# Two reorderings in a four-layer kernel: the ternary linear's third block, and the first gate and up products of a SwiGLU

## The chip, the cores and the metric

The kernel runs on one core of a Trainium2 chip. The metric is the device time of one execution in microseconds (us). The time of a kernel is the median of its runs. One execution was taken by the hardware profiler, and all rows that are shown come from it.

## The reference

The input is 2 x 1024 tokens of 512 channels, in float32. Four layers follow one another, each as `x = layernorm(x + layer(x))`:

1. a state-space layer (input projection, short causal convolution, scan, gated output projection),
2. a ternary linear layer: `out = (x @ W) * scale`, with W of -1, 0 and 1, then each row scaled by tanh of its norm and clipped to norm 0.99,
3. a recurrence layer:
   `y = gelu(x @ w_y + b_y)`, `c = causal_conv(x @ w_x + b_x)`, `i = sigmoid(c @ w_ig + b_ig)`, `a = exp(-8 * sigmoid(c @ w_ag + b_ag) * softplus(a_param))`, `h[t] = a[t] * h[t-1] + sqrt(1 - a[t]^2) * i[t] * c[t]`, `out = (h * y) @ w_out + b_out`,
4. a SwiGLU layer with integer weights (less 128, scaled per output channel): `out = (silu(x @ Wg) * (x @ Wu)) @ Wd`, hidden size 2048.

The change touches the border between layers 2 and 3, and the one between layers 3 and 4.

## The kernel before, in words

**Blocks.** The 2048 tokens are four blocks of 512 (`NBLK` = 4, two per sequence). `X[b]` holds block b in SBUF, 128 tokens x 4 groups `j` x 512 channels. The 512 channels are four chunks `k` of 128. A product needs the block with channels on the partitions, so each block is first transposed by TensorE: 16 transposes of 128 x 128 into four PSUM tiles `pt`, each copied to SBUF by ScalarE. A product against float32 data is a matmul that appears as two instructions in the profile. Layers 2 and 4 use a cheaper form (`exact`): the activations are split into a rounded high part (a cast on ScalarE) and the low rest (a subtraction on VectorE), and each k takes one matmul of each part.

**PSUM.** All PSUM tiles come from one pool of eight banks, `ps.tile([P, 512], F32, tag="mm")`. Every product, every transposed chunk and every accumulating output takes one bank until its last reader is done.

**Order.** Python traces the program, and the framework's scheduler then fixes one order per engine. In a model of the run, each engine takes, of the instructions that are ready and can get their buffer, the one that was traced first. An instruction traced earlier thus has a higher rank, but a later one that is ready goes ahead of it when it isn't. On the chip each engine keeps the order that was fixed and waits on semaphores. Generators with `yield` and the helper `weave(main, fill, plan)` set the order of tracing: after each step of `main`, as many steps of `fill` as `plan` says.

**Border of layers 2 and 3.** `linear(b)` is the ternary layer of block b. Its four steps are: transposes (L219), high cast `wu` (L223) and low part `wd` (L224); two of the four token groups, each eight matmuls (L896), a scaling on VectorE (L900) and a square with row sum on ScalarE (L902); the other two groups; and norm, tanh (L910) and the update of `X[b]` (L906 to L920) with a layernorm on GpSimd (L244). The pieces `wu` and `wd` have one buffer, so a block's casts wait until the block before has been multiplied. `linear(0)` and `linear(1)` are woven into the end of layer 1, whose last block is stored to DRAM (L735) and read back (L935). `branches(b)` begins layer 3 for block b: transposes (L219) with copies by ScalarE (L228), then four products with `w_x` (L947) each followed by bias, convolution and carry, then four with `w_y` and a gelu. Its transposed block lies in memory that layer 1 held. Here `branches(0)` is the `main` of a `weave` and `linear(2)`, `linear(3)` the `fill`, one step of fill after each of the first eight steps.

**Border of layers 3 and 4.** For each block, `recurrence(b)` does the two gate products, the activations and the scan; `project_back(b)` multiplies the result by `w_out` (32 matmul instructions, L1024, into four banks `po`), adds the bias (`r`, L1029, VectorE) and adds it to `X[b]` (L1030, GpSimd), with a layernorm for all but the last block. In the loop `project_back(b - 1)` stands behind `recurrence(b)`. Behind the loop stand `by_channel(0, X, pieces)`, the transposes (L877), high casts (L880) and low parts `lo` (L882) of block 0 for the SwiGLU, and `project_back(3)`. Then the pool of layer 4 is opened, and `hidden(0)` multiplies block 0 by the first 128 columns of gate and up (16 matmuls, L1098, into two banks `pgu`), with silu (L1105), product (L1107) and its split for the down-projection (L1121).

All of this is traced twice, `later_layers(True)` and, behind a test of the weights, `later_layers(False)`; with these inputs the second is jumped over.

Of the kernel before, what the change touches and what calls it, by code (L numbers as in the profile page):

```python
# [16 lines left out]
P = 128  # L17
# [3 lines left out]
NK = D // P  # L21
# [16 lines left out]
def model_kernel(ctx: ExitStack, tc: tile.TileContext, t: dict, out: bass.AP):  # L38
    nc = tc.nc
# [15 lines left out]
    def bank(name):  # L55
        return ps.tile([P, 512], F32, tag="mm", name=name)
# [198 lines left out]
    def weave(main, fill, plan, rest=True):  # L255

        for i, _ in enumerate(main):
            for _ in range(plan[i] if i < len(plan) else 0):
                next(fill, None)
        for _ in fill if rest else ():  # L260
            pass
# [475 lines left out]
    H, before, st = None, None, {}  # L737
    own, coming = head(0, st), {}
    g, ahead = gates(0, st), head(1, coming)
# [8 lines left out]
    for b in range(NBLK):  # L748
        if b:
            g, coming = gates(b, st), {}  # L750
# [54 lines left out]
    GK = GW // P  # L805
# [3 lines left out]
    def later_layers(exact, last=None):  # L809
# [62 lines left out]
        def by_channel(b, X, pieces):  # L872

            for k in range(NK):
                pt = bank("pt")
                for j in range(NJ):
                    nc.tensor.transpose(  # L877
                        pt[:, j * P : (j + 1) * P], X[b][:, j, k * P : (k + 1) * P], ident
                    )
                nc.scalar.copy(pieces[0][:, k, :], pt)  # L880
                if exact:
                    nc.vector.tensor_tensor(  # L882
                        pieces[1][:, k, :], pt, pieces[0][:, k, :].bitcast(F32), ALU.subtract
                    )

        def linear(b):

            xT = transposed(ep, b, X, tags=("wu0", "wd0") if exact else ("wu0",), split=exact)
            yield
            o = ep.tile([P, NJ, D], F32, tag="wF", name="o" + suffix)  # L890
            ssq = sp.tile([P, NJ], F32, tag="ssq", name="ssq")
            for j in range(NJ):
                po = bank("po")
                for k in range(NK):
                    for x in xT:
                        nc.tensor.matmul(  # L896
                            po, x[:, k, j * P : (j + 1) * P], wf[:, k, :],
                            start=(k == 0 and x is xT[0]), stop=(k == NK - 1 and x is xT[-1]),
                        )
                nc.vector.tensor_tensor(o[:, j, :], po, f0s, ALU.mult)  # L900
                junk = ep.tile([P, GW], mybir.dt.bfloat16, tag="junk", name="junk2")
                nc.scalar.activation(junk, o[:, j, :], AF.Square, accum_out=ssq[:, j : j + 1])  # L902
                if j % 2:
                    yield
            norm = sp.tile([P, NJ], F32, tag="norm", name="norm")
            nc.scalar.activation(norm, ssq, AF.Sqrt)  # L906
            v = sp.tile([P, NJ], F32, tag="v", name="v")
            nc.vector.tensor_scalar(v, norm, 1e-7, None, ALU.max)
            f = sp.tile([P, NJ], F32, tag="f", name="f")
            nc.scalar.activation(f, v, AF.Tanh)  # L910
            nc.vector.tensor_scalar(v, v, 1e-7, None, ALU.add)
            nc.vector.reciprocal(v, v)
            nc.vector.tensor_tensor(f, f, v, ALU.mult)
            nc.vector.tensor_tensor(norm, norm, f, ALU.mult)
            nc.vector.tensor_scalar(norm, norm, 1e-7, None, ALU.max)
            nc.vector.reciprocal(norm, norm)
            nc.vector.tensor_scalar(norm, norm, 0.99, 1.0, ALU.mult, ALU.min)
            nc.vector.tensor_tensor(f, f, norm, ALU.mult)
            for j in range(NJ):
                nc.vector.scalar_tensor_tensor(  # L920
                    X[b][:, j, :], o[:, j, :], f[:, j : j + 1], X[b][:, j, :],
                    ALU.mult, ALU.add,
                )
            layernorm(X[b], engine=nc.gpsimd)
            yield
# [10 lines left out]
        for i, name in ((2, "w_ig"), (3, "w_ag"), (4, "w_out")):  # L936
            nc.sync.dma_start(w1[:, i], w_sources[name])


        with tc.tile_pool(name="rec" + suffix, bufs=1, side="right", reuse_waits="tile") as rp:  # L940
            carry = rp.tile([P, NK, 3], F32, tag="carry", name="carry1")
# [11 lines left out]
            def branches(b, st):  # L953

                xT = transposed(rp, b, X, by_act=True)[0]
                yield
                cv = st["cv"] = rp.tile([P, NK, TB], F32, tag="cv", name="cv", bufs=2)
                y = st["y"] = rp.tile([P, NK, TB], F32, tag="y", name="y", bufs=2)
                for m in range(NK):
                    pm = product(0, m, xT)  # L960
                    xpad = rp.tile([P, 3 + TB], F32, tag="xpad", name="xpad1", bufs=2)
                    if b % BPS == 0:
                        nc.gpsimd.memset(xpad[:, 0:3], 0.0)
                    else:
                        nc.gpsimd.tensor_copy(xpad[:, 0:3], carry[:, m, :])
                    nc.scalar.activation(xpad[:, 3:], pm, AF.Identity, bias=bx[:, m : m + 1])
                    if b % BPS < BPS - 1:
                        nc.gpsimd.tensor_copy(carry[:, m, :], xpad[:, TB : TB + 3])
                    nc.vector.tensor_scalar(
                        cv[:, m, :], xpad[:, 3:], cw1[:, m, 3:4], cb1[:, m : m + 1],  # L970
                        ALU.mult, ALU.add,
                    )
                    causal_conv(cv[:, m, :], xpad, cw1[:, m, :])
                    yield
                for m in range(NK):
                    pm = product(1, m, xT)
                    nc.scalar.activation(y[:, m, :], pm, AF.Gelu, bias=by[:, m : m + 1])
                    yield
# [41 lines left out]
            def project_back(b, y):  # L1020
                for j in range(NJ):
                    po = bank("po")
                    for k in range(NK):
                        nc.tensor.matmul(  # L1024
                            po, y[:, k, j * P : (j + 1) * P], w1[:, 4, k, :],
                            start=(k == 0), stop=(k == NK - 1),
                        )
                    r = rp.tile([P, D], F32, tag="t2", name="r1", bufs=4)
                    nc.vector.tensor_tensor(r, po, bout, ALU.add)  # L1029
                    nc.gpsimd.tensor_tensor(X[b][:, j, :], X[b][:, j, :], r, ALU.add)  # L1030

                if b + 1 < NBLK:
                    layernorm(X[b])

            st = {}
            weave(branches(0, st), itertools.chain(linear(2), linear(3)), (1,) * 8)
            bout = row("L1_attn_b_out", D, c1, nc.sync, "scale")
            wg, wu, wd = ([weights(ep, which, 0)] for which in ("wg", "wu", "wd"))
            ys = []
# [11 lines left out]
                for tag in (("wF", "lo") if exact else ("wF",))  # L1051
            ]
            by_channel(0, X, pieces)
            project_back(NBLK - 1, ys[-1])
            dsc = row("L1_ffn_down_scale", D, c1, nc.sync, "scale")

# [3 lines left out]
        with tc.tile_pool(name="ffn" + suffix, bufs=1, side="right", reuse_waits="tile") as fp:  # L1060
# [26 lines left out]
                            i += 1  # L1087
                        yield

            def hidden(m):  # L1090

                g, cols = m // GK, slice(m % GK * P, m % GK * P + P)
                pgu = []
                for w in (wg, wu):
                    pm = bank("pgu")
                    for k in range(NK):
                        for x in pieces:
                            nc.tensor.matmul(  # L1098
                                pm, w[g][:, k, cols], x[:, k, :],
                                start=(k == 0 and x is pieces[0]),  # L1100
                                stop=(k == NK - 1 and x is pieces[-1]),
                            )
                    pgu.append(pm)
                sg = fp.tile([P, TB], F32, tag="sg", name="sg", bufs=2)
                nc.scalar.activation(sg, pgu[0], AF.Silu, scale=gs[:, m : m + 1])  # L1105
                h = fp.tile([P, TB], F32, tag="h", name="h", bufs=2 if exact else 3)
                nc.vector.scalar_tensor_tensor(  # L1107
                    h, pgu[1], us[:, m : m + 1], sg, ALU.mult, ALU.mult
                )
                if not exact:  # L1110
                    return [h]
                hh = fp.tile([P, TB], F32R, tag="hh", name="hh", bufs=4)
                nc.scalar.copy(hh, h)  # L1113
                hl = fp.tile([P, TB], F32R, tag="hl", name="hl", bufs=4)
                nc.vector.tensor_tensor(hl, h, hh.bitcast(F32), ALU.subtract)
                return [hh, hl]
# [6 lines left out]
                            start=(m == 0 and x is h[0]), stop=(m == NF - 1 and x is h[-1]),  # L1123
                        )

            ready, check = [hidden(0)], squares()
            loads = itertools.chain(*(group(g) for g in range(1, NG)))
            for b in range(NBLK):
                final = b + 1 == NBLK
# [124 lines left out]
```

## Time and profile before

| what | us |
|---|---|
| median of 3 runs | 1148.89 |
| lowest and highest run | 1146.79, 1148.90 |
| the profiled execution | 1149.05 |
| its span, first to last instruction | 1147.2 |
| TensorE busy in the span | 1118.7 (98%) |
| VectorE busy | 678.9 (59%) |
| ScalarE busy | 459.0 (40%) |
| GpSimd busy | 361.9 (32%) |

The profiled execution's time is 1.85 us over its span. In the rows, PE is TensorE's matmuls, PEld its weight loads, DVE VectorE, ACT ScalarE, POOL GpSimd and SP the engine that issues most DMAs; `L947` is line 947 of the kernel. A timeline row has the start in us from the begin of the span, the time in us, engine, line, operation, output and inputs, shapes and count; in brackets stands the idle time of the engine ahead of it and what ended that. Neighbouring instructions of one kind are merged into one row. The end of a matmul is modelled, so that rows on PE overlap a little; the step from start to start is the price of one.

### The profile page before, as it was taken

How to read it: one execution, taken by the hardware profiler on the slowest of the kernel's cores; microseconds unless marked ns; L12 is line 12 of the kernel's file. 1: busy time of each engine (PE TensorE's matmuls, PEld its weight loads, DVE VectorE, ACT ScalarE, POOL GpSimd, SP SyncE). 2: the span in 40 equal slices, each digit the busy share in tenths (PEclk: the TensorE clock that was granted, in tenths of full speed). 3: DMA queues.
4: the chain of work that ended last, by engine and by line, in shares of the span. 5: the costliest groups of instructions: out<-in, count | busy, mean ns of one | idle time of the engine just before them, and what ended most of it. 6: DMA issues, size and time to landing. Idle time of an engine off the chain costs nothing.

```text
span 1147.2 us, 12259 instructions
## 1 busy us (share of the span) xinstructions
PE 1118.7 (98%) x4614; PEld 684.2 (60%) x4614; DVE 678.9 (59%) x1228; ACT 459.0 (40%) x700; POOL 361.9 (32%) x347
## 2 busy tenths in 40 slices
PE   8989999999999999999999999999999999999995
PEld 5455445445544555654444444448888888888884
DVE  4887896696769676863717237083328765225224
ACT  3343544463454233566654372533223223223222
POOL 1446472555248240556123212237401001001002
PEclk9999999999999999999999999999999999999998
DMA  8004002400220038112000000004501001001001
GB/s 316 20 14 167 2 1 89 166 0 37 69 113 0 38 144 234 74 31 89 1 1 0 1 0 1 0 1 128 175 1 38 1 1 37 1 1 37 1 1 40
DMA packets 32699, 59.22 MB, mean 52 GB/s; under 512 B 11808, under 2 KB 12608, under 8 KB 30072
## 3 DMA queue, kind: packets, MB, share of 16 engines
q1 hardware_dynamic: 31608, 58.21, 14.5%
q8 instruction: 38, 0.62, 0.2%
q14 instruction: 29, 0.24, 0.1%
q10 hardware_dynamic: 864, 0.14, 0.1%
q0 software_dynamic: 160, 0.01, 0.0%
HBM read 49.47 MB, written 8.68 MB: 51 GB/s over the span
## 4 chain that ended last, share of the span: by engine, by line
PE 84%; DVE 10%; ACT 4%; issue 1%; POOL 0%; DVEq 0%; ACTq 0%; POOLq 0%
PE pgu L1098 21%; PE p L947 17%; PE po L1121 10%; PE pg L323 9%; PE px L323 7%; PE po L715 6%; PE po L1024 4%; PE py L650 3%; DVE acc L251 2%; PE po L896 2%; DVE L L522 2%; PE pxt L619 1%; PE pt L219 1%; DVE xc L700 1%; PE py L642 1%
## 5 line engine op out<-in xcount | busy, mean ns | idle before, releaser
L1107 DVE SCALAR_TENSOR_TENSOR h<-pgu,L_ffn_up_scale,sg 128x512 f32<-128x512 f32 x64 | 47.9, 749 | 147.7 <-PE pgu L1098 143.7
L323 PE MATMUL px<-xT,w_in 128*128 128x512 f32 x256 | 114.6, 597 | 0.2 <-DVE over L509 0.2
L537 POOL TENSOR_TENSOR L<-L,gm 128x512 f32<-128x512 f32 x64 | 93.5, 1490 | 67.0 <-DVE bdec L532 29.4
L715 PE MATMUL po<-w_out,xc 128*128 128x512 f32 x256 | 112.5, 593 | 2.1 <-DVE L L522 2.1
L947 PE MATMUL p<-xT,w 128*128 128x512 f32 x256 | 112.1, 592 | 1.4 <-ACT xT L228 1.4
L323 PE MATMUL pg<-xT,w_in 128*128 128x512 f32 x256 | 113.4, 594 | 0.0
L947 PE MATMUL p<-cv,w 128*128 128x512 f32 x256 | 111.0, 592 | 0.0
L1121 PE MATMUL po<-wd,hh 128*128 128x512 f32 x256 | 101.3, 396 | 0.0
L1098 PE MATMUL pgu<-wF__4424,wg 128*128 128x512 f32 x256 | 101.2, 396 | 0.0
L1121 PE MATMUL po<-wd,hl 128*128 128x512 f32 x256 | 101.0, 394 | 0.0
L1098 PE MATMUL pgu<-lo__4425,wg 128*128 128x512 f32 x256 | 100.7, 393 | 0.0
L1098 PE MATMUL pgu<-lo__4425,wu 128*128 128x512 f32 x256 | 100.7, 393 | 0.0
L1098 PE MATMUL pgu<-wF__4424,wu 128*128 128x512 f32 x256 | 100.7, 393 | 0.0
L1105 ACT ACTIVATE sg<-pgu,L_ffn_gate_scale 128x512 f32<-128x512 f32 x64 | 44.0, 688 | 133.1 <-PE pgu L1098 133.0
L1113 ACT CAST hh<-h 128x512 fp32r<-128x512 f32 x64 | 39.7, 621 | 117.5 <-DVE h L1107 117.3
L715 PEld LDWEIGHTS po<-w_out,xc 128*128 128x128 f32 x256 | 48.4, 190 | 63.1 <-issue 55.7
L947 PEld LDWEIGHTS p<-cv,w 128*128 128x128 f32 x256 | 48.4, 190 | 59.8 <-issue 58.6
L947 PEld LDWEIGHTS p<-xT,w 128*128 128x128 f32 x256 | 48.4, 190 | 58.8 <-issue 55.3
L323 PEld LDWEIGHTS px<-xT,w_in 128*128 128x128 f32 x256 | 47.6, 190 | 57.8 <-issue 56.3
L1195 POOL TENSOR_TENSOR x<-x,r 128x512 f32<-128x512 f32 x12 | 15.2, 1294 | 205.9 <-DVE r L1194 205.9
L323 PEld LDWEIGHTS pg<-xT,w_in 128*128 128x128 f32 x256 | 47.4, 190 | 54.3 <-issue 53.7
L251 DVE SCALAR_TENSOR_TENSOR acc<-xpad,cols,acc 128x512 f32<-128x512 f32 x72 | 67.4, 939 | 18.5 <-ACT acc L293 14.8
(268 smaller groups left out, 1937.2 us busy)
## 6 DMA issues: line engine op xcount, KB each, us to landing
L<-decays SPq DMA_DIRECT2D x12, 1024.0 KB, 9.1
x_mid<-x SPq DMA_DIRECT2D x4, 1024.0 KB, 3.8
x<-x_mid SPq DMA_DIRECT2D x4, 1024.0 KB, 6.8
st<-in_L_ffn_gate_w_dram SPq DMA_DIRECT2D x8, 512.0 KB, 4.5
st<-in_L_ffn_up_w_dram SPq DMA_DIRECT2D x8, 512.0 KB, 4.1
st<-in_L_ffn_down_w_dram SPq DMA_DIRECT2D x8, 512.0 KB, 3.6
x<-_attn_hidden_states_dram SPq DMA_DIRECT2D x3, 1024.0 KB, 9.9
out_dram<-x SPq DMA_DIRECT2D x3, 1024.0 KB, 4.4
```

The costliest lines, as they stand in the source:

```text
L251: nc.vector.scalar_tensor_tensor(acc, xpad[:, k : k + TB], w[:, k : k + 1], acc, ALU.mult, ALU.add)
L323: nc.tensor.matmul(pm[:n, :], w_in[:, k, lo : lo + n], xT[:, k, :], start=(k == 0), stop=(k == NK - 1),)
L537: nc.gpsimd.tensor_tensor(L[:, h, :], L[:, h, :], st["gm"], ALU.mult)
L650: nc.tensor.matmul(pys[i][hh * HD : (hh + 1) * HD, q, :], dtx[q][:, 2 * i + hh, :], L[:, h, s], start=(first and q == 0), stop=(q == 1), s ...
L715: nc.tensor.matmul(po, xc[:, m, j * P : (j + 1) * P], w_out[:, m, :], start=(m == 0), stop=(m == NX - 1),)
L947: nc.tensor.matmul(pm, w1[:, i, k, m * P : (m + 1) * P], rhs[:, k, :], start=(k == 0), stop=(k == NK - 1),)
L1024: nc.tensor.matmul(po, y[:, k, j * P : (j + 1) * P], w1[:, 4, k, :], start=(k == 0), stop=(k == NK - 1),)
L1098: nc.tensor.matmul(pm, w[g][:, k, cols], x[:, k, :], start=(k == 0 and x is pieces[0]), stop=(k == NK - 1 and x is pieces[-1]),)
L1105: nc.scalar.activation(sg, pgu[0], AF.Silu, scale=gs[:, m : m + 1])
L1107: nc.vector.scalar_tensor_tensor(h, pgu[1], us[:, m : m + 1], sg, ALU.mult, ALU.mult)
L1113: nc.scalar.copy(hh, h)
L1121: nc.tensor.matmul(po[j], x[:, j * P : (j + 1) * P], wd[m // GK][:, m % GK, :], start=(m == 0 and x is h[0]), stop=(m == NF - 1 and x is h ...
```

## The change

It does two things to the order of tracing. In front of the weave of `branches(0)`, one step is taken from the fill, so that the first step of `linear(2)` is traced ahead of the first step of `branches(0)`, and every later step of the two `linear` blocks comes one step of `branches(0)` earlier. And the matmuls of gate and up are taken out of `hidden` into a function `gate_up`, which is called for m = 0 between `by_channel(0)` and `project_back(3)`; `hidden(0)` then gets the two banks handed over. No operation is added or removed.

```diff
+        def gate_up(m):
+            g, cols = m // GK, slice(m % GK * P, m % GK * P + P)
+            pgu = []
+            for w in (wg, wu):
+                pm = bank("pgu")
+                for k in range(NK):
+                    for x in pieces:
+                        nc.tensor.matmul(
+                            pm, w[g][:, k, cols], x[:, k, :],
+                            start=(k == 0 and x is pieces[0]),
+                            stop=(k == NK - 1 and x is pieces[-1]),
+                        )
+                pgu.append(pm)
+            return pgu
...
             st = {}
-            weave(branches(0, st), itertools.chain(linear(2), linear(3)), (1,) * 8)
+            rest = itertools.chain(linear(2), linear(3))
+            next(rest)
+            weave(branches(0, st), rest, (1,) * 8)
...
             by_channel(0, X, pieces)
+
+            first_hidden = gate_up(0)
             project_back(NBLK - 1, ys[-1])
...
-            def hidden(m):
+            def hidden(m, pgu=None):
+
+                pgu = pgu or gate_up(m)
...
-            ready, check = [hidden(0)], squares()
+            ready, check = [hidden(0, first_hidden)], squares()
```

More of the change, by code (lines that the diff above doesn't have):

```diff
@@ L1088, in squares @@
                         yield
-            def hidden(m):
[L1092 to L1103, printed above, removed]
+            def hidden(m, pgu=None):
+                pgu = pgu or gate_up(m)
                 sg = fp.tile([P, TB], F32, tag="sg", name="sg", bufs=2)
```

## The prediction

> **What bounds the kernel now.** The page first: TensorE is busy for 98% of the span, no other engine for over 60% (PEld overlaps PE).
>
> ```profile
> PE 1118.7 (98%) x4614; PEld 684.2 (60%) x4614; DVE 678.9 (59%) x1228; ACT 459.0 (40%) x700; POOL 361.9 (32%) x347
> ```
>
> So an edit that only moves work can gain no more than TensorE's waits. Next, the waits of TensorE: place, what it waited for, us in total, times, longest. In the two stages touched there are these:
>
> ```profile
> PE po L1024 <- DVE r L1029: 1.7, 1, 1.7
> PE p L947 <- ACT xT L228: 1.4, 1, 1.4
> PE po L896 <- DVE wd L224: 0.9, 2, 0.8
> PE pt L219 <- POOL xpad L963: 0.4, 1, 0.4
> ```
>
> That is 4.4 us, 0.38% of the time: the ceiling. What comes later has no slack to swallow a delay: in the table by stage the SwiGLU reads (length, then busy us of PE, PEld, DVE, ACT, POOL; then the granted clock)
>
> ```profile
> 800.00:900.00 100.00, 100.00 (x441) 81.56 (x441) 49.33 (x96) 27.77 (x42) 20.98 (x28) 1.00 0.19 65
> ```
>
> 100.00 of 100.00, so a microsecond lost or won on TensorE ahead of it reaches the end in full.
>
> The timeline by engine around the first stage, TensorE's rows, then ScalarE's (start, length, line; in brackets the idle time before):
>
> ```profile
> 458.90 1.17 PE L896 MATMUL po<-wfr,wu 128*128 128x512 f32 x4
> 460.22 0.50 PE L896 MATMUL po<-wfr,wd 128*128 128x512 f32 x1 [0.15 <-DVE wd L224]
> ...
> 466.73 0.49 PE L219 MATMUL pt<-ident,x 128*128 128x128 f32 x3
> 467.63 3.38 PE L219 MATMUL pt<-ident,x 128*128 128x128 f32 x29 [0.41 <-POOL xpad L963]
> 472.43 3.70 PE L947 MATMUL p<-xT,w 128*128 128x512 f32 x8 [1.41 <-ACT xT L228]
> ```
>
> ```profile
> 469.43 1.28 ACT L910 ACT_TABLE_LOAD   x1
> 470.72 0.20 ACT L910 ACTIVATE f<-v 128x4 f32<-128x4 f32 x1
> 470.83 1.05 ACT L223 CAST wu<-pt 128x512 fp32r<-128x512 f32 x2
> 471.78 2.06 ACT L228 COPY xT<-pt 128x512 f32<-128x512 f32 x4
> ```
>
> Two things are to be seen. The four `wu` matmuls at 458.90 run in a row although each group alternates `wu` and `wd`: the order on TensorE is built by readiness, a group is opened with its high part and then waits for its low part. And the 32 transposes (16 of `branches(0)`, 16 of `linear(2)`) end near 471.0, after which TensorE has nothing until the copy of `xT`. That copy starts at 471.78 because its memory held a token block: SyncE issued the store of the last block (L735) at 467.03, and only at 471.57 the load behind it (L935), which must wait for that store.
>
> The timeline of all engines around the second stage:
>
> ```profile
> 756.25 1.91 PE L877 MATMUL pt<-ident,x 128*128 128x128 f32 x16
> ...
> 759.10 0.67 DVE L1029 TENSOR_TENSOR r<-po,L_attn_b_out 128x512 f32<-128x512 f32 x1
> 759.82 14.00 PE L1024 MATMUL po<-w,y 128*128 128x512 f32 x32 [1.66 <-DVE r L1029]
> ...
> 760.27 1.94 DVE L1029 TENSOR_TENSOR r<-po,L_attn_b_out 128x512 f32<-128x512 f32 x3
> ...
> 765.90 0.66 DVE L882 TENSOR_TENSOR lo__4425<-pt,wF__4424 128x512 fp32r<-128x512 f32 x1
> ...
> 769.62 0.68 DVE L882 TENSOR_TENSOR lo__4425<-pt,wF__4424 128x512 fp32r<-128x512 f32 x1
> ...
> 773.25 0.80 PE L1098 MATMUL pgu<-wF__4424,wg 128*128 128x512 f32 x1
> ```
>
> The 1.66 us are a wait for a PSUM bank. All eight are taken: four `po` of block 2, which VectorE reads only from 759.10, and four `pt` of `by_channel`, which the subtraction L882 frees from 766.56. The first reader ends at 759.77 and the out-projection of block 3 starts at 759.82.
>
> **The change, part by part.** No instruction is added or removed and no DMA is moved; nothing passes anything on SP's or POOL's queue. The sum is made against the profiled execution, 1149.05 us (span 1147.2 and 1.85 around it); the median of the runs is 0.16 lower, and the same difference is applied to it.
>
> *Part 1, `linear(2)` one step earlier.* Its 16 transposes, four casts (L223) and four subtractions (L224) now rank ahead of the transposes and copies of `branches(0)`, and each later pair of its matmul groups one product earlier.
> (a) Its transposes read X[2], whose load was issued at 427.52, not X[0], which GpSimd finishes at 467.58. 16 of them at 0.11 us (29 take 3.38 with the pipeline's tail) cover 466.73 to 468.5; the 0.41 wait goes: -0.4.
> (b) The 1.41 wait can be filled by matmuls of `linear(2)`, 32 at 0.23 us (the step between rows of L896), if pieces and banks are there. Banks: eight transposed tiles hold all eight, and the first one comes free with the first L224. Pieces: ScalarE is held by the table load and tanh of `linear(1)` until 470.83. If a cast or two slips in ahead, at 467.2 or between norm and tanh, most of the gap is filled; if not, the first low piece is ready at about 472.1, as before, and nothing is won, while the four casts (2.05 us) in front push the copies back by up to 1.05. Bounds -1.4 and +1.0; I take half of the gap, -0.7.
> (c) In-order waits for low pieces: the same pattern cost 0.15 at 460.22 and 0.79 at 501.10. With four casts and subtractions entering VectorE's chain of `linear(1)` (L908 to L920, nothing on TensorE waits for it) I add 0.5, between these two; bounds 0 and 0.9. The 0.79 itself, in `linear(3)`, I leave as it is: +-0.8.
> Part 1: -0.4 - 0.7 + 0.5 = -0.6 us.
>
> *Part 2, gate and up of the first hidden chunk ahead of `project_back(3)`.* 16 matmuls at 0.23 us, 3.6 us, move from 773.25 to behind the transposes, and TensorE's work stays the same. They want two banks, and they want the low pieces `lo`, which VectorE makes at 765.90 to 770.3, since the r of block 2, its statistics and its normalising rank ahead. What they can do before is one matmul per group, the high part of the first k, as at 458.90. Nothing fills the 1.66 us, for no bank is free. But then gate takes the bank of 759.77, up that of the second r (760.27 + 0.68 = 760.95), and `po` of block 3 starts with the third, at 760.88 + 0.68 = 761.56, so at 761.6 instead of 759.82: 1.78 late, of which 2 x 0.23 is work done ahead: +1.3. The two groups stay open until about 770; the out-projection needs its second bank at 765.0 (fourth r, 762.2) and its third at 768.5 (L882, from 766.56): no further wait.
> The other 14 matmuls are placed among the 32 of `po` where the scheduler's model has `lo` ready. VectorE stood still twice for 0.45 us in 763 to 765.2, waiting for GpSimd's additions, and took no `lo` there though the casts were done by 758.9: the order has no such holes, so on the chip `lo` comes up to 0.9 later than its place. In-order TensorE then waits 0 to 0.9: +0.5. What waits behind it is `po`, and behind that all of the SwiGLU.
> Part 2: +1.3 + 0.5 = +1.8 us.
>
> *The clock.* One row speaks against the change. After a stretch with 0.97 of 3.41 us of matmuls (a wait of 2.44) the clock fell to half for 3.41 us:
>
> ```profile
> 72.15:75.56 3.41, 0.97 (x11) 0.61 (x10) 3.20 (x7) 0.83 (x2) 1.27 (x2) 1.00 0.27 77
> 75.56:78.97 3.41, 3.41 (x42) 3.05 (x42) 2.65 (x7) 0.00 (x0) 0.81 (x1) 0.50 0.00 0
> ```
>
> In the changed kernel 758.16 to 761.6 holds 3.4 us with two matmuls, 0.46 us. The Trainium skill, "TensorE: Matmul & The Clock Gate", summary section "Why this matters for your kernels", asks for no idle gap over about 3 us, one idle window sending the clock to half; the window is free-running, so its phase differs from run to run. By that rule two matmuls inside keep it from being an idle gap: 0. By the row a window needs less than 0.97 busy: then the window may overhang the gap by 0.5 us on either side, some 1.0 of 3.41 phases, and it costs half of 3.41, 1.7 us. I take 0 for the sum, since most phases miss, and 1.7 as a case.
>
> Sum: -0.6 + 1.8 = +1.2. 1149.05 + 1.2 = 1150.25 profiled, 1150.1 on the median. Hidden edits: the fallback copy of the layers is changed too and is not executed; the earlier silu (0.69) and product (0.75) feed a down-projection that is not waited for today.
>
> **The rivals.** *Clock* (slower): as the sum, with one half-clock window at 758 to 762 paid: +2.9, 1151.8. It decides from a window with under 0.97 us of matmuls. For: the row at 72.15. Against: the present gap of 1.66 never brought it, and the phase has to fit. *Gap filled* (faster): a bank is free after all, or block 2's r comes earlier, so that gate and up fit into the 1.66 while part 1 takes its two waits whole: down to -1.66 - 1.82 = -3.5; with two thirds of it -2.4, 1146.5. For: TensorE idles just there. Against: the wait's releaser is r, and four plus four banks are eight. *Not as it says*: the freed bank goes to the older waiter, `po`, and gate and up fall in where they were: part 2 is 0, part 1 -0.6, 1148.3.
>
> **How the numbers follow.** About 0.2%, 2.3 us, is what a measurement of this kernel tells from no change. The sum holds with 0.48 (own range 1148.3 to 1151.8: within 0.37, slower 0.11), clock 0.30 (slower 0.24, within 0.06), gap filled 0.12 (faster 0.10, within 0.02), not as it says 0.10 (within 0.08, faster 0.02). Together 0.12, 0.53, 0.35. The range runs from 1147.0, near the gap filled, to 1152.9, clock with the upper bounds of the waits.
>
> **What would show it.** Right: the wait of L1024 for r near 3 us in place of 1.7, with one or two L1098 rows inside it; L1098 rows mixed among L1024 up to 770, some waiting for `lo`; the wait for xT under 1.4 and L896 rows before the first L947; the one on POOL gone. Wrong: L1098 rows filling 758 to 760, L1024 starting at 759.8 as before, or a wait of several us on L224 or L882. A second half-clock window marks the rival.

## The result and the profile after

| | before | after |
|---|---|---|
| median, us | 1148.89 (7 runs) | 1153.77 (7 runs) |
| lowest, highest | 1146.52, 1150.41 | 1151.53, 1157.59 |
| ratio after to before | | 1.0052, 95% interval 1.0034 to 1.0071 |
| profiled execution, its span | 1149.05, 1147.2 | 1156.42, 1154.3 |

The changed kernel is slower by 4.9 us, or 0.5%. The forecast was +1.2 us, with a range that ended at 1152.9, so the measured 1153.77 lies above it.

The profiled executions differ by more, 7.1 us of span. Of this, 1.84 us are there before either edit acts: the first matmul of `linear(0)` starts at 437.63 instead of 435.78. The execution of after had one more half-clock stretch early (from 40.2 us on, 3.41 us long), which would account for most of it. Neither edit touches what is traced up to there, and the runs of both kernels lie in steps of about this size. I therefore take times between two places of one trace, and compare these.

| from, to | before | after | difference |
|---|---|---|---|
| last matmul of `linear(1)`, first gate product of `recurrence(0)` | 51.03 | 52.34 | +1.3 |
| from there to the first down-projection | 263.41 | 267.27 | +3.9 |
| from there to the end | 366.23 | 366.30 | +0.1 |

Together +5.2 in this execution, against 4.9 between the medians. In the view of TensorE's waits, the rows on `xT` (1.4) and on POOL (0.4) are gone, and so is `po` on `r`; in their place stand

```profile
PE pgu L947 <- DVE r L1045: 2.4, 2, 1.8
PE po L896 <- DVE wd L224: 2.3, 2, 2.2
PE po L1130 <- ACT hh L1122: 1.1, 1, 1.1
```

(After the edit, L947 is gate and up, L963 the product with `w_x`, L1040 the out-projection, L1045 `r`, L1130 the down-projection. In the experiments the lines shift again; the names of the tiles stay.)

**First stage.** TensorE's timeline of after, then its row of before for the same place in `linear(3)`:

```profile
468.57 3.65 PE L219 MATMUL pt<-ident,x 128*128 128x128 f32 x32
471.98 0.48 PE L896 MATMUL po<-wfr,wu 128*128 128x512 f32 x1
...
499.69 0.50 PE L896 MATMUL po<-wfr,wd 128*128 128x512 f32 x1 [2.19 <-DVE wd L224]
```

```profile
501.10 0.50 PE L896 MATMUL po<-wfr,wd 128*128 128x512 f32 x1 [0.79 <-DVE wd L224]
```

All 32 transposes run in one row, and matmuls of `linear(2)` follow at once: the whole 1.8 us is won. ScalarE had made the casts ahead of its table load:

```profile
471.25 0.58 ACT L223 CAST wu<-pt 128x512 fp32r<-128x512 f32 x1
471.72 0.21 ACT L906 ACTIVATE norm<-ssq 128x4 f32<-128x4 f32 x1
471.83 1.07 ACT L223 CAST wu<-pt 128x512 fp32r<-128x512 f32 x2
472.91 1.28 ACT L910 ACT_TABLE_LOAD   x1
```

Then `linear(3)` waits 2.2 us for its low part, where it waited 0.79.

**Second stage.** TensorE, then VectorE, then ScalarE of after, and last ScalarE of before:

```profile
759.39 1.91 PE L877 MATMUL pt<-ident,x 128*128 128x128 f32 x16
763.05 0.47 PE L947 MATMUL pgu<-wF__4424,wg 128*128 128x512 f32 x1 [1.75 <-DVE r L1045]
764.16 0.79 PE L947 MATMUL pgu<-wF__4424,wu 128*128 128x512 f32 x1 [0.64 <-DVE r L1045]
764.76 5.79 PE L1040 MATMUL po<-w,y 128*128 128x512 f32 x10
769.99 0.79 PE L947 MATMUL pgu<-lo__4425,wg 128*128 128x512 f32 x1
...
787.95 1.19 PE L1130 MATMUL po<-wd,hh 128*128 128x512 f32 x4 [1.09 <-ACT hh L1122]
```

```profile
783.25 0.69 DVE L1045 TENSOR_TENSOR r<-po,L_attn_b_out 128x512 f32<-128x512 f32 x1 [0.46 <-PE po L1040]
785.34 0.69 DVE L238 BATCH_NORM_STATS2 st<-x 128x6 f32<-128x512 f32 x1 [1.39 <-POOL x L1046]
786.06 0.18 DVE L239 BATCH_NORM_AGGREGATE mv<-st 128x2 f32<-128x6 f32 x1
786.16 1.57 DVE L1116 SCALAR_TENSOR_TENSOR h<-pgu,L_ffn_up_scale,sg 128x512 f32<-128x512 f32 x2
```

```profile
785.09 0.69 ACT L1114 ACTIVATE sg<-pgu,L_ffn_gate_scale 128x512 f32<-128x512 f32 x1 [9.97 <-PE pgu L947]
785.80 1.28 ACT L241 ACT_TABLE_LOAD   x1
787.09 0.30 ACT L241 ACTIVATE rs<-mv,eps 128x4 f32<-128x4 f32 x1
787.30 1.15 ACT L1122 CAST hh<-h 128x512 fp32r<-128x512 f32 x2
```

```profile
779.46 0.62 ACT L1113 CAST hh<-h 128x512 fp32r<-128x512 f32 x1 [0.36 <-DVE h L1107]
780.10 1.28 ACT L1105 ACT_TABLE_LOAD   x1
781.39 0.69 ACT L1105 ACTIVATE sg<-pgu,L_ffn_gate_scale 128x512 f32<-128x512 f32 x1
```

The high part of gate and up, one matmul each, goes into the first two banks, as foreseen. The silu of the first chunk was done at 775.1, yet its product `h` stands on VectorE behind the last statistics of block 3 and goes together with that of the second chunk (x2). On ScalarE the cast `hh` stands behind the second silu (785.09), a table load and the square root of the layernorm; before, it stood ahead of the second silu (779.46, 781.39).

**Clock.** The table by stage, in the boundaries in which the clock changes:

```profile
497.61:501.03 3.42, 1.27 (x5) 0.75 (x5) 3.42 (x11) 0.30 (x1) 0.00 (x0) 1.00 0.00 0
501.03:504.44 3.41, 3.41 (x7) 2.04 (x7) 2.90 (x5) 0.00 (x0) 3.29 (x2) 0.50 0.00 0
760.44:763.85 3.41, 1.33 (x9) 0.81 (x7) 3.37 (x5) 1.64 (x4) 0.86 (x1) 1.00 0.00 0
763.85:767.27 3.42, 3.11 (x4) 1.46 (x5) 2.97 (x7) 0.00 (x0) 3.42 (x4) 0.50 0.02 5
```

Two stretches at half clock follow windows in which TensorE was busy for 1.27 and 1.33 us, each with a wait in it that the edit brought. The first one can be priced from this profile: the first stage is 1.31 us longer although TensorE idles 0.35 us less in it (0.07 + 2.19 against 0.41 + 1.41 + 0.79). The other 1.66 us are about half of 3.41.

In each profile the clock changes at whole multiples of 3.413 us from one another (in after at 40.23, 77.78, 501.03 and 763.85), so that TensorE's work can be read window by window. In all 14 profiles, behind the first 10 us and apart from the windows near 36 to 43 us that the last section tells of, every window at full clock with up to 1.56 us of matmuls was followed by half clock, and none with 1.65 or more.

### The profile page after: what moved, and what is told of

Its sections match the earlier page's. It is cut to its first block, busy times and chain, and to the rows that moved or that the text cites. A ratio compares the mean times of both kernels' runs of the same rounds, so it can differ in the third digit from the quotient of the medians.

```text
span 1154.3 us, 12256 instructions
## 1 busy us (share of the span) xinstructions
PE 1123.9 (97%) x4614; PEld 685.2 (59%) x4614; DVE 680.0 (59%) x1228; ACT 456.1 (40%) x698; POOL 361.2 (31%) x347
## 4 chain that ended last, share of the span: by engine, by line
PE 82%; DVE 11%; ACT 4%; issue 1%; DMA 1%; POOL 0%; DVEq 0%; ACTq 0%; POOLq 0%
PE pgu L947 20%; PE p L963 17%; PE po L1130 10%; PE pg L323 9%; PE px L323 7%; PE po L715 6%; PE po L1040 4%; PE py L650 3%; DVE acc L251 2%; DVE L L522 1%; PE po L896 1%; PE pxt L619 1%; PE pt L219 1%; DVE xc L700 1%; DVE st L238 1%
## 5 line engine op out<-in xcount | busy, mean ns | idle before, releaser
L963 PE MATMUL p<-xT,w 128*128 128x512 f32 x256 | 112.3, 595 | 0.0
L963 PE MATMUL p<-cv,w 128*128 128x512 f32 x256 | 111.0, 592 | 0.0
L947 PE MATMUL pgu<-wF__4424,wg 128*128 128x512 f32 x256 | 101.4, 396 | 1.8 <-DVE r L1045 1.8
L1130 PE MATMUL po<-wd,hh 128*128 128x512 f32 x256 | 100.9, 396 | 1.1 <-ACT hh L1122 1.1
L947 PE MATMUL pgu<-wF__4424,wu 128*128 128x512 f32 x256 | 101.1, 395 | 0.6 <-DVE r L1045 0.6
L947 PE MATMUL pgu<-lo__4425,wg 128*128 128x512 f32 x256 | 101.5, 397 | 0.0
L947 PE MATMUL pgu<-lo__4425,wu 128*128 128x512 f32 x256 | 100.7, 393 | 0.0
L1130 PE MATMUL po<-wd,hl 128*128 128x512 f32 x256 | 100.5, 394 | 0.0
L963 PEld LDWEIGHTS p<-cv,w 128*128 128x128 f32 x256 | 48.4, 190 | 59.8 <-issue 58.6
L963 PEld LDWEIGHTS p<-xT,w 128*128 128x128 f32 x256 | 48.8, 191 | 58.5 <-issue 56.7
L522 DVE TENSOR_TENSOR_SCAN L<-pl,id 128x512 f32<-128x512 f32 x64 | 75.1, 1208 | 6.4 <-ACT pl L516 3.5
```

Of the source, the lines that this page charges most:

```text
L522: nc.vector.tensor_tensor_scan(L[:, h, :], pl, id4.rearrange("p j t -> p (j t)"), 0.0, ALU.mult, ALU.add)
L947: nc.tensor.matmul(pm, w[g][:, k, cols], x[:, k, :], start=(k == 0 and x is pieces[0]), stop=(k == NK - 1 and x is pieces[-1]),)
L963: nc.tensor.matmul(pm, w1[:, i, k, m * P : (m + 1) * P], rhs[:, k, :], start=(k == 0), stop=(k == NK - 1),)
L1130: nc.tensor.matmul(po[j], x[:, j * P : (j + 1) * P], wd[m // GK][:, m % GK, :], start=(m == 0 and x is h[0]), stop=(m == NF - 1 and x is h ...
```

## The experiments

All ratios are to the kernel before, in runs on the same chip, with the 95% interval. The kernel before has a median of 1149.35 us beside experiments 1, 2 and `early_pieces`, 1148.54 beside 3 and `gate_early`, and 1149.29 beside 5. "First stage", "second stage" and "last stage" are the three differences of the table above, from each kernel's profile.

**1. Each part alone.** `linear_only` has the first of these two edits, `gate_only` the second:

```diff
+            rest = itertools.chain(linear(2), linear(3))
+            next(rest)
-            weave(branches(0, st), itertools.chain(linear(2), linear(3)), (1,) * 8)
+            weave(branches(0, st), rest, (1,) * 8)
...
+            first_hidden = gate_up(0)
             project_back(NBLK - 1, ys[-1])
...
-            ready, check = [hidden(0)], squares()
+            ready, check = [hidden(0, first_hidden)], squares()
```

> Part 1 alone: one step of the fill taken ahead of the weave, gate and up left in hidden(0). Theory (waits plus clock): the waits on POOL and on the xT copy vanish (-1.8 us), the wait of linear(3) for its low part grows from 0.8 to 2.2 us (+1.4), and in part of the runs that longer wait is followed by 3.4 us at half clock (1.7 us, in about half of them): together -0.4 to +1.3, +0.4 us in the mean. Rival (the loss is all in part 2): -0.4 us, with as many half-clock stretches as before. Rival (part 1 carries the loss): +3 us or more.

> Part 2 alone: gate_up(0) ahead of project_back(3), the weave as before. Theory: 1.3 us for the banks, 1.1 us for the late h of the first hidden chunk, and a half-clock stretch behind the gap at about 760 us in more than half of the runs (1.7 us each): +2.4 to +4.1, about +3.5 us. Rival (clock stretches are chance and have nothing to do with the change): +2.4 us and a mean granted clock no lower than that of the kernel before. The profile should show L947 waiting 1.7 and 0.6 us for r, and L1130 waiting about 1.1 us for hh.

`linear_only`: 1151.15, ratio 1.0014 (1.0008 to 1.0021), first stage +1.05, a half-clock stretch at 498.6 behind a window with 1.22 us of matmuls. That is more than the +0.4 that I expected in the mean. `gate_only`: 1155.43, ratio 1.0043 (1.0030 to 1.0056), second stage +4.3, stretch at 764.0, waits of 2.4 for `r` and 1.1 for `hh`. Both parts cost time, and the second costs most of it.

**2. Which of the two linear blocks brings the wait.** In `linear2_only`, `linear(3)` keeps its old place:

```diff
+            rest = itertools.chain(linear(2), linear(3))
+            next(rest)
-            weave(branches(0, st), itertools.chain(linear(2), linear(3)), (1,) * 8)
+            weave(branches(0, st), rest, (1, 1, 1, 0, 1, 1, 1, 1))
```

> Part 1 for linear(2) alone: the step ahead of the weave stays, but the plan is (1,1,1,0,1,1,1,1), so that linear(3) stands where it stood before. Theory: the waits on POOL and xT vanish (-1.8 us) and the wait of linear(3) for its low part stays near the 0.8 us of before: -1.8 us, no further half-clock stretch. Rival (any order with linear(2) in front makes VectorE late for linear(3)): a wait of about 2 us on L224 stays, -0.4 us or worse.

1150.23, ratio 1.0004 (0.9995 to 1.0012), first stage +1.1. The wait stays, 2.4 us, with a half-clock stretch behind it, and so my expectation failed. It isn't `linear(3)` that was moved too far. In after, VectorE works without a hole from 489.7 to 499 (update of block 2, statistics, convolution) and makes the low part at 498.98:

```profile
493.21 2.74 DVE L920 SCALAR_TENSOR_TENSOR x<-o,f,x 128x512 f32<-128x512 f32 x4
495.86 1.28 DVE L238 BATCH_NORM_STATS2 st<-x 128x6 f32<-128x512 f32 x2
...
498.45 0.52 DVE L985 TENSOR_SCALAR cv<-xpad,cw,L_attn_conv_b 128x512 f32<-128x512 f32 x1
498.88 0.18 DVE L239 BATCH_NORM_AGGREGATE mv<-st 128x2 f32<-128x6 f32 x1
498.98 0.66 DVE L224 TENSOR_TENSOR wd<-pt,wu 128x512 fp32r<-128x512 f32 x1
```

Measured from the end of `linear(1)`, the wait ends 3.2 us earlier than before (31.35 us instead of 34.60), but TensorE begins it 4.6 us earlier: 1.8 by the waits that it lost, the rest because some matmuls that stood ahead of it now stand behind. With VectorE full, what TensorE wins in front of it is mostly given back. In `linear2_only` VectorE is full as well and does more of the convolution ahead of the low part, which comes at 503.27. No run took work off VectorE here, so this cause is read from the profiles and not tested.

**3. A half-clock stretch filled, at each place.** Matmuls that are repeated and overwritten by what stands behind them: 17 of the first `wu` of `linear(3)` in `linear_filled` (on `linear_only`), 4 + 1 at gate and up in `after_filled` (on the changed kernel), ten of the identity near 72 us in `before_warm` (on the kernel before). In this order:

```diff
                 po = bank("po")
+                for _ in range(17 if exact and b == 3 and j == 0 else 0):
+                    nc.tensor.matmul(
+                        po, xT[0][:, 0, j * P : (j + 1) * P], wf[:, 0, :], start=True, stop=True
+                    )
...
                 pm = bank("pgu")
+                for _ in range(fills.pop(0) if fills else 0):
+                    nc.tensor.matmul(
+                        pm, w[g][:, 0, cols], pieces[0][:, 0, :], start=True, stop=True
+                    )
...
-            first_hidden = gate_up(0)
+            first_hidden = gate_up(0, [4, 1])
...
             for i in range(4):
+                for _ in range(10 if warm and q == 1 and i == 3 else 0):
+                    nc.tensor.matmul(pt[:, 3 * P :], ident, ident, start=True, stop=True)
```

> The kernel before with linear(2) one step earlier, and linear(3)'s first high-part matmul repeated 17 times (3.9 us, overwritten by the group) where TensorE takes a product and then waits 2.2 us for the low part. Theory (part 1 wins 0.7 us in its waits and loses it again to a half-clock stretch behind that wait): the wait for wd falls under 0.5 us, the stretch near 500 is gone, and the median is 0.5 to 1.0 us under the kernel before, about 1148.5. Rival (the repeats are work added in full, because the product that they displace waits for nothing): the stretch is gone, yet the time is that of part 1 alone, 1151, or up to 2 us above it.

> The changed kernel with the first matmul of gate repeated four times more and that of up once, each ahead of its group and overwritten by it: 1.15 us of matmuls in the 0.64 us between the two banks and in the 0.37 us behind the second. Theory (what the early gate and up cost beyond their waits is a half-clock stretch, brought by a 3.41 us window with too few matmuls): the waits stay as they were (2.4 us on r, 1.1 us on hh), the profile shows no half-clock stretch near 764, and the median falls by up to 1.7 us against the changed kernel, to about 1152.0. Rival (the cost is in the waits alone, or the single gap of 1.75 us is enough for the clock to fall): no gain, 1153.8, or 0.1 to 0.3 more for the added matmuls, with the stretch near 764 still there.

> The kernel before with ten 128x128 matmuls of the identity added (overwritten by the transpose behind them) in the 2.4 us in which TensorE waits for xc near 72 to 75. Theory (a half-clock stretch of 3.41 us follows a window with too few matmuls and costs 1.7 us wherever it falls): the stretch near 75.6 is gone and the time falls by 1.7 us less what the added matmuls delay, 0 to 0.4: 1147.4 to 1147.8. Rival (the stretch does not depend on the matmuls of the window ahead, or costs nothing, since what follows waits for other things): no change, 1149.3.

`linear_filled`: 1152.07, ratio 1.0031 (1.0021 to 1.0041). The stretch near 500 is gone and the wait is 1.3 in three pieces in the view of the waits, but the first stage is +3.3: the rival was right that the repeats (17 x 0.23 = 3.9) are paid in full. Less these 3.9 it is -0.6, near the -0.7 that `linear_only` shows less one stretch (1.05 - 1.7). So the stretch near 500 costs its 1.7 us in full.

`after_filled`: 1155.14, ratio 1.0052 (1.0038 to 1.0067): no gain. Its profile has no stretch at 764, as the table by stage and TensorE's timeline show:

```profile
759.50:762.90 3.40, 1.65 (x15) 1.40 (x13) 3.36 (x5) 2.05 (x4) 0.40 (x1) 1.00 0.00 0
762.90:766.30 3.40, 3.40 (x12) 1.92 (x11) 3.33 (x7) 0.00 (x0) 3.40 (x3) 1.00 0.02 5
```

```profile
769.31 0.50 PE L951 MATMUL pgu<-lo__4425,wg 128*128 128x512 f32 x1 [0.47 <-DVE lo__4425 L882]
769.64 0.40 PE L951 MATMUL pgu<-wF__4424,wg 128*128 128x512 f32 x1
769.97 0.50 PE L951 MATMUL pgu<-lo__4425,wg 128*128 128x512 f32 x1
```

But the repeats are not shown to have removed it. Of the rows of the table, the first is the window ahead; it begins 3.1 us before the first gate matmul. In `after_add_dve` (experiment 5), which has the same gap and no repeats, the window begins 3.1 us before it too, holds as much work, and is not followed by half clock either. In after and `gate_only` it begins 2.6 and 1.1 us before, and is. `gate_only`, then `after_add_dve`:

```profile
760.58:763.99 3.41, 1.56 (x4) 0.73 (x5) 3.41 (x7) 0.14 (x1) 2.37 (x2) 1.00 0.02 5
763.99:767.40 3.41, 3.41 (x6) 1.33 (x5) 2.51 (x7) 0.00 (x0) 2.96 (x3) 0.50 0.00 0
```

```profile
757.64:761.05 3.41, 1.66 (x13) 1.24 (x11) 3.37 (x5) 2.05 (x4) 0.43 (x1) 1.00 0.00 0
761.05:764.47 3.42, 2.69 (x7) 1.24 (x7) 3.26 (x7) 0.00 (x0) 3.42 (x3) 1.00 0.02 5
```

So whether this gap brings the stretch depends on where the window falls. These profiles also give the price. `after_add_dve` waits for `r` and `hh` as after does (2.4 and 1.1 us), and without the stretch its second stage is +3.5, against +3.9 in after and +4.3 in `gate_only` with it. At full clock TensorE comes early for the low parts, waits 0.44 us there (0.47 in `after_filled`), and then takes a pair of matmuls each 0.66 us, the pace at which VectorE makes `lo` (L882, 0.66 each), in place of 0.46. In `after_filled` the first `lo` matmul begins 6.74 us behind the first gate matmul, in after 6.94. So the stretch at 764 lies over a wait that is there without it, and costs 0.3 to 0.8 us, not the 1.7 of my theory.

`before_warm`: 1149.92, ratio 1.0008 (0.9998 to 1.0018). Its profile has no stretch near 75, but one at 39.3 and a new wait of 1.3 us for `dtx` behind the added matmuls. Three other profiles without these added matmuls (`after_filled`, `gate_early`, `after_h_early`) have a stretch near 39 and none near 75 as well. So it tells neither what removes a stretch nor its price.

**4. Banks.** In `early_pieces` (on the kernel before) and `gate_early` (on part 2 alone), the pieces of the SwiGLU input are traced ahead of the last recurrence, so that four banks are free (the same lines behind the loop are taken out):

```diff
+                if b + 1 == NBLK:
+                    pieces = [
+                        ep.tile([P, NK, TB], WT, tag=tag, name=f"{tag}_{suffix}")
+                        for tag in (("wF", "lo") if exact else ("wF",))
+                    ]
+                    by_channel(0, X, pieces)
                 recurrence(b, st["cv"], ys[b], coming)
```

> The kernel before, with by_channel(0) (transposes, casts, low parts of block 0) traced ahead of recurrence(3), so that its four PSUM banks are free again long before project_back(3); gate and up stay in hidden(0). Theory (the 1.7 us wait ahead of project_back(3) is a shortage of banks): that wait vanishes, -1.7 us. Rival (VectorE's chain of the last recurrence is what TensorE waits for): the wait stays, now for y (L1018), and the time is the same or, with four subtractions more in front of that chain, up to 2 us longer.

> Part 2 alone, with the pieces of the SwiGLU input (by_channel of block 0) traced ahead of the last recurrence instead of behind it, so that the four transposed tiles have left their banks when gate and up want theirs. Theory (the static cost of part 2 is the lack of banks, and the out-projection behind it waits for y when banks are free): no wait on r ahead of gate and up or of the last out-projection (2.4 us in part 2 alone); the 16 matmuls, 3.7 us, stand in the 1.4 us in which TensorE waited for y; the wait for hh may stay at about 1 us. Sum against the kernel before: -1.4 to -1.7 + 1.1, with no half-clock stretch near 764: 1148.3 to 1149. Rival (moving gate and up costs by itself, whatever the banks): slower than the kernel before by 1 us or more, 1150.5 to 1153.

`early_pieces`: 1150.75, ratio 1.0005 (0.9997 to 1.0013). The wait on `r` is gone and one of 1.4 us for `y`, the recurrence's last output, stands in its place: the rival was right. `gate_early`: 1153.05, ratio 1.0034 (1.0020 to 1.0047). Now all 16 matmuls fit in ahead of the last out-projection, and neither `r` nor `y` is waited for. But

```profile
PE po L1129 <- ACT hh L1121: 3.8, 1, 3.8
```

and the second stage is still +2.1. Behind that wait the clock is at half for two windows, from 783.3 to 790.1, of which the first, with 2.07 us of matmuls, did not bring it back to full; the last stage is +2.8. (The profiled run is the slowest of nine, 1155.78.) VectorE makes `h` behind block 3's last statistics here too (783.20, behind 782.37). What the free banks won came back at the first down-projection, and more.

**5. The first hidden chunk's order.** `after_h_early`: in the changed kernel silu and product of the first chunk are traced behind `gate_up(0)`, into a weight staging tile that is free there; cast and low part stay. `after_add_dve`: in the changed kernel block 3's addition is on VectorE. `gate_h_early` and `gate_h_early_add_dve` are `gate_early` with the first of these edits, and with both.

The diff shows the calls; `gated` is a new function that holds the silu and the product of `hidden`.

```diff
-            first_hidden = gate_up(0)
+            first_hidden = gated(0, gate_up(0), ep, "0")
...
-                    nc.gpsimd.tensor_tensor(X[b][:, j, :], X[b][:, j, :], r, ALU.add)
+                    adder = nc.gpsimd if b + 1 < NBLK else nc.vector
+                    adder.tensor_tensor(X[b][:, j, :], X[b][:, j, :], r, ALU.add)
```

> The changed kernel with silu and product of the first hidden chunk (h(0)) also traced ahead of the last out-projection, in a free weight staging tile, so that h(0) stands on VectorE ahead of the bias additions and statistics of block 3; cast, low part and down-projection stay where they are. Theory (half of the cover of h(0) was moved away: the 1.1 us wait of the first down-projection is VectorE's order, r and statistics of block 3 ahead of h(0)): the wait for hh goes, nothing over 0.3 us comes in its place, and the time falls by 1.1 us: about 1152.7. Rival (what is late is the end of the chain r, addition on GpSimd, statistics itself, so the low part hl, which still stands behind it, is waited for instead): the same 1153.8.

> The changed kernel with the addition to X of block 3, behind the last out-projection, on VectorE (0.7 us each) instead of GpSimd (1.27 us and two hand-overs), h(0) left behind the statistics. Theory (the wait for hh is the length of the chain behind the last token group: r 0.69, 1.39 until the addition is done, statistics 0.69, h 0.75, hh 0.6, of which 3.6 us of gate and up(1) cover the first part): the chain is 0.7 us shorter, the wait for hh falls from 1.1 to about 0.4, the time to about 1153.1. Rival (hh waits for something else than VectorE's order, such as the table load on ScalarE ahead of its cast): wait and time as in the changed kernel, 1.1 and 1153.8.

> Part 2 alone with the pieces of the SwiGLU input traced ahead of the last recurrence (so that banks are free) and h(0) ahead of the last out-projection. Theory: the 3.8 us wait for hh of the kernel with early pieces was VectorE's order alone; hh is ready, and the low part hl, still behind the statistics of block 3, is waited for: 1.5 to 2.2 us in place of 3.8, with no wait on r. Sum against the kernel before: -1.7 + 1.9, 1148.9, plus the half-clock stretch behind that wait in some runs: 1149 to 1150.6. Rival (TensorE's order, not VectorE's, keeps the down-projection late): a wait of 3 to 4 us stays, 1151 to 1153.

> The kernel above with block 3's addition on VectorE too. Theory (with banks free, h(0) ahead and the chain behind the last token group shorter, nothing is left to wait for): no wait on r, y, hh or hl over 0.4 us between 757 and 785, and the 1.7 us that TensorE waits there in the kernel before are won: 1147.1, a version faster than both. Rival (a wait returns each time one is removed, here for hl or for the statistics that now stand in VectorE's way): 1148.5 to 1150.

`after_h_early`: 1154.36, ratio 1.0043 (1.0028 to 1.0057). The wait for `hh` is gone, nothing follows, and the second stage is +2.3. This profile has no stretch at 764, so it is to be set beside `after_add_dve` (+3.5) and not after (+3.9): 1.2 us won, the size of the wait. The ratio's interval overlaps that of after, so the gain is shown in the profile only.

`after_add_dve`: 1155.33, ratio 1.0046 (1.0030 to 1.0062). The wait is 1.1 as before: the rival was right. ScalarE:

```profile
782.38 0.69 ACT L1115 ACTIVATE sg<-pgu,L_ffn_gate_scale 128x512 f32<-128x512 f32 x1 [9.98 <-PE pgu L947]
783.09 1.28 ACT L241 ACT_TABLE_LOAD   x1
784.38 0.30 ACT L241 ACTIVATE rs<-mv,eps 128x4 f32<-128x4 f32 x1
784.59 1.16 ACT L1123 CAST hh<-h 128x512 fp32r<-128x512 f32 x2
```

From the second silu to the cast it is 2.21 us, to the hundredth what it is in after (785.09 to 787.30), although `h` was ready at 783.92. What is late is the cast, in ScalarE's order behind that silu and a table load.

`gate_h_early`: 1153.52, ratio 1.0033 (1.0022 to 1.0045). The first `hh` matmul starts 1.9 us earlier than before, measured from the recurrence, without a wait; then the low part, still behind the statistics of block 3, is waited for:

```profile
784.21 0.80 PE L1138 MATMUL po<-wd,hl 128*128 128x512 f32 x1 [3.12 <-DVE hl L1132]
```

I had expected 1.5 to 2.2. A half-clock stretch follows here too, and the last stage is +4.6.

`gate_h_early_add_dve`: 1149.10, ratio 0.9999 (0.9990 to 1.0008). The second stage is -1.9, the whole wait of before. Of it 1.1 us is lost again within 18 us, at two places:

```profile
780.87 0.40 PE L1139 MATMUL po<-wd,hh 128*128 128x512 f32 x1
781.49 0.50 PE L1139 MATMUL po<-wd,hl 128*128 128x512 f32 x1 [0.22 <-DVE hl L1133]
...
796.82 0.40 PE L947 MATMUL pgu<-lo__4278,wu 128*128 128x512 f32 x1
797.40 0.50 PE L947 MATMUL pgu<-wF__4277,wu 128*128 128x512 f32 x1 [0.18 <-POOL wu L851]
```

The brackets show 0.2 us each, since the modelled end of the matmul ahead covers the rest. Counted from start to start against before, it is 0.5 us at `hl` and 0.6 us at the weight `wu`, whose staging tile `h` had borrowed. A further 0.3 us lies behind the last matmul; its cause stays open. The time is the rival's, 1148.5 to 1150. So the best version found equals the kernel before, and none beats it.

## Why the prediction was wrong

It said +1.2 us, as -0.6 and +1.8. By its steps:

- *Part 1, (a) and (b)*: direction right. Both waits went whole, -1.8, where I had taken -0.4 and half of 1.4. Casts did slip in ahead of the table load. The reading that the copy of `xT` started at 471.78 because of its memory is not shown: ScalarE's rows have no idle time from 468.45 on, and the copy starts when the two casts ahead of it end.
- *Part 1, (c)*: the step "the 0.79 itself, in `linear(3)`, I leave as it is" failed. It became 2.2, +1.4, outside the +-0.8. I had not read what VectorE does there: it is full, and so, as far as the profiles show, an earlier TensorE waits for it. The +0.5 for `linear(2)` did not come as a wait. Waits alone: -1.8 + 1.4 = -0.4.
- *Clock*: the step that took it as 0 failed, and I had weighed it at one place only. The stretch near 500 lies behind the wait just named, in all six profiles with `linear(2)` ahead and nothing filled in there, and makes the first stage +1.3 instead of -0.4. That is the largest term I missed: 1.7. The threshold was also misread from one row: a window with 0.97 us of matmuls that brings half clock does not show that one with more is safe. Here windows with up to 1.56 us brought it, and those with 1.65 us, or with 1.81 as at the old gap (758.22 to 761.63 before), did not. The Trainium skill's "TensorE: Matmul & The Clock Gate", section "Why this matters for your kernels", says to leave no idle gap over about 3 us; the gaps here were 1.75 and 2.2 us, and the measurement decides.
- *Part 2, banks*: right in mechanism and size. From the first transpose to the out-projection it is 3.57 us before and 5.37 after: 1.80 late less 0.46 done ahead, +1.3.
- *Part 2, `lo`*: right in mechanism, at the upper bound in size. I had 0.5 (0 to 0.9) for one in-order wait. In `after_add_dve`, without a stretch, the first `lo` matmul comes 0.6 us late and the next pairs lose 0.3 us more: 0.9. In after and `gate_only` the half-clock stretch lies over it, no wait on `lo` is seen, and the two together cost 0.3 to 0.8 us more than that.
- *Part 2, "a down-projection that is not waited for today"*: the step that put this at nothing failed. The wait is 1.1 us, 1.2 from start to start. What hid the first chunk's silu, product and cast were two chunks of gate and up, 7.3 us, behind the out-projection. The edit moved one of them away, and with 3.6 us left the cast, behind ScalarE's second silu and table load, is late. I had named the cover and not its price when half of it goes, though the rows were there.

For part 2 without a stretch these terms give 1.3 + 0.9 + 1.2 = 3.4, against the +3.5 of `after_add_dve`.

The rival *clock* named the mechanism, at a place where it cost little and came in two of the four unfilled profiles with this gap; the place where it cost 1.7 us was not among the cases. *Gap filled* and *not as it says* fell: no bank was free, and the freed one went to gate.

What stays open: why the scheduler puts the first product behind block 3's statistics on VectorE though its inputs are there some 11 us earlier, and whether less work on VectorE near 490 to 499 us would keep part 1's gain.

## What to carry to other kernels

Work that is moved forward on the busiest engine leaves a hole in the cover where it stood: list who was hidden by it, on every engine's own queue, and what it costs them. A wait that is removed ahead of another engine's full stretch comes back behind it; here 1.4 of 1.8 us did. And a new wait of about 2 us on TensorE is to be priced with the half-clock stretch that may follow it, at each place where the change can bring one. One profile without the stretch does not show that it was removed: compare where the windows fall.

## What the hardware showed unexpectedly

A stretch at half clock (3.41 us) makes the work in it late by about 1.7 us where TensorE is the limit (near 500), but it costs only 0.3 to 0.8 us where TensorE would have waited for VectorE anyway (764). And a window that is full can be followed by half clock too: in after, 36.82 to 40.23 is 3.23 us busy of 3.41, nearly all with matmuls of 16 or 48 rows, and the next window has 0.50. Whether the shape is the cause no run here shows.
